# TensorE in a loop of 12 slots, with GpSimd's copies as its only wait

## The chip, the cores and the metric

The kernel runs on one core of one Trainium2 chip. The time is device microseconds of a whole execution. The execution from which the profile comes has its own time, which stands beside its span in the table below.

## The reference

128 batches of a 128 x 1024 float32 array are each multiplied by one of eight 128 x 128 matrices, picked by an index for each batch, and the product is added to the input.

```python
def reference(x, itok_B_0_7, L0_cond_weights):
    w = L0_cond_weights[itok_B_0_7]              # 128 x 128 x 128 from 8 x 128 x 128
    return x + jnp.einsum('bct,bcd->bdt', x, w)  # x: 128 x 128 x 1024 float32
```

The input and the output have 67.1 MB each, so some 134 MB go through the transfer engines.

## The kernel before

Two batches (G = 2) make one step of the main loop, 64 steps in all. A step has a slot `xs[k]` of 1 MB in SBUF (128 partitions x 2 x 1024 float32), and there are SLOTS = 23 slots, used in turn (k = i % SLOTS). The sum is written into the slot itself, so a slot is taken from the load of x until the store of the result has landed.

All instructions are written out in full, and the order on each engine is the order of the text. Semaphores alone tie the engines together:

- SyncE (SP) issues the load of the eight matrices (L130) and then 128 loads of 512 KB, two for each step, by the helper `transfer` (L57). For the first 23 steps a load waits until the load three steps earlier has landed (LEAD = 3); from then on it waits until the store out of the same slot has landed (`s_slot[k]`, which counts both loads and the store of each turn).
- GpSimd (POOL) reads eight indices at a time into registers (L155) and copies the matrix of each batch from `w_all` into one of four buffers `ws` (L165). It waits for `s_product`, so that a buffer is not overwritten while TensorE may still read it; so it runs up to four batches ahead.
- TensorE (PE) waits in each step for the loads of the slot (`s_slot[k]`), for the addition two steps earlier, which frees one of the two PSUM tiles (`s_added`), and in each batch for the copy of its matrix (`s_copied`). Then it does two products of 128x512 for each batch (L171). Its whole program, 256 products, is written out one after the other. Three products on zeros stand ahead of it (L114).
- VectorE (DVE) adds PSUM to the slot, one addition of 128x2048 for each step (L181). At the start it clamps the indices (L121 to L125).
- ScalarE (ACT) issues one store of 1 MB for each step, after the addition (L57 again, seen as ACTq).

The helper puts the transfers of SP and of ACT on one hardware queue each; in the profile q1 has the loads and q10 the stores. After its loads SP waits until the last store of every slot has landed (L192), and with that the kernel ends.

Of the kernel before, what the change touches and what calls it, by code (L numbers as in the profile page):

```python
# [1 line left out]

# [4 lines left out]

F32 = mybir.dt.float32
I32 = mybir.dt.int32
ALU = mybir.AluOpType


G = 2

N = 512  # L30

SLOTS = 23

W_SLOTS = 4
P_SLOTS = 2

R = 8
DMA = 16

TURN = DMA * (G + 1)  # L40

LEAD = 3

IDLE = 3

ROWS = 4
QUEUES = {mybir.EngineType.SP: "qSPDynamicHW", mybir.EngineType.Activation: "qActDynamicHW"}


def transfer(nc, engine, out, in_):  # L50

    later, nc._always_lower_symbolic_ap = nc._always_lower_symbolic_ap, False
    ins, outs = engine.lower_ap_dma(in_), engine.lower_ap_dma(out)
    nc._always_lower_symbolic_ap = later
    return engine.add_instruction(  # L57
        mybir.InstDMACopy(
            name=nc.get_next_instruction_name(),
            engine=engine.engine,  # L60
            ins=ins,
            outs=outs,
            mode="Copy",
            cce_op=ALU.bypass,
            queue=QUEUES[engine.engine],
        )
    )


@with_exitstack  # L70
def kernel(
    ctx: ExitStack,
    tc: tile.TileContext,
    x: bass.AP,
    subjects: bass.AP,
    weights: bass.AP,
    out: bass.AP,
):
    nc = tc.nc
    B, C, T = x.shape  # L80
    S, _, D = weights.shape
    NT = B // G

    def sbuf(name, *shape, dtype=F32):
        return ctx.enter_context(nc.sbuf_tensor(name, list(shape), dtype)).ap()

    given, near, wrap, index = (
        sbuf(name, 1, B, dtype=I32) for name in ("given", "near", "wrap", "index")
    )
    w_all = sbuf("w_all", C, S, D)  # L90
    ws = [sbuf(f"w{i}", C, 1, D) for i in range(W_SLOTS)]
    zeros = sbuf("zeros", C, N)
    xs = [sbuf(f"x{i}", C, G, T) for i in range(SLOTS)]
    ps = [
        ctx.enter_context(nc.psum_tensor(f"ps{i}", [D, G, T], F32)).ap() for i in range(P_SLOTS)
    ]

    s_given = tc.alloc_semaphore("s_given")
    s_wall = tc.alloc_semaphore("s_wall")
    s_index = tc.alloc_semaphore("s_index")  # L100
    s_zeros = tc.alloc_semaphore("s_zeros")
    s_copied = tc.alloc_semaphore("s_copied")
    s_product = tc.alloc_semaphore("s_product")
    s_added = tc.alloc_semaphore("s_added")
    s_slot = [tc.alloc_semaphore(f"s_slot{i}") for i in range(SLOTS)]

    with tc.tile_critical():  # L107

        nc.scalar.dma_start(given, subjects.rearrange("(o b) -> o b", o=1)).then_inc(s_given, DMA)

        nc.vector.memset(zeros, 0.0).then_inc(s_zeros, 1)  # L111
        nc.tensor.wait_ge(s_zeros, 1)
        for _ in range(IDLE):
            nc.tensor.matmul(  # L114
                ps[P_SLOTS - 1][:, G - 1, :N], zeros[:, :D], zeros, start=True, stop=True
            )

        nc.vector.wait_ge(s_given, DMA)  # L120
        nc.vector.tensor_scalar(near, given, -S, S - 1, ALU.max, ALU.min).then_inc(s_index, 1)  # L121
        nc.vector.wait_ge(s_index, 1)
        nc.vector.tensor_scalar(wrap, near, 0, S, ALU.is_lt, ALU.mult).then_inc(s_index, 1)  # L123
        nc.vector.wait_ge(s_index, 2)
        nc.vector.tensor_tensor(index, near, wrap, ALU.add).then_inc(s_index, 1)  # L125
        nc.gpsimd.wait_ge(s_index, 3)

        nc.sync.dma_start(w_all, weights.rearrange("s c d -> c s d")).then_inc(s_wall, DMA)  # L130
        for i in range(NT):
            k, turn = i % SLOTS, i // SLOTS
            if turn:
                nc.sync.wait_ge(s_slot[k], TURN * turn)
            elif i >= LEAD:
                nc.sync.wait_ge(s_slot[k - LEAD], DMA * G)
            for g in range(G):
                transfer(
                    nc,
                    nc.sync,  # L140
                    xs[k][:, g, :],
                    x[i * G + g].rearrange("(a r) t -> a (r t)", r=ROWS),
                ).then_inc(s_slot[k], DMA)

        nc.gpsimd.wait_ge(s_wall, DMA)
        for i in range(NT):
            k, turn = i % SLOTS, i // SLOTS
            p = ps[i % P_SLOTS]
            nc.tensor.wait_ge(s_slot[k], TURN * turn + DMA * G)
            if i >= P_SLOTS:  # L150
                nc.tensor.wait_ge(s_added, i - P_SLOTS + 1)
            for g in range(G):
                b = i * G + g
                if b % R == 0:
                    _, subject = nc.values_load_multi_w_load_instructions(  # L155
                        index[0:1, b : b + R],
                        engines=[mybir.EngineType.Pool],
                        min_val=0,
                        max_val=S - 1,
                        skip_runtime_bounds_check_because="the index is clamped on the chip above",  # L160
                    )
                w = ws[b % W_SLOTS]
                if b >= W_SLOTS:
                    nc.gpsimd.wait_ge(s_product, b - W_SLOTS + 1)
                nc.gpsimd.tensor_copy(w, w_all[:, bass.ds(subject[b % R], 1), :]).then_inc(  # L165
                    s_copied, 1
                )

                nc.tensor.wait_ge(s_copied, b + 1)
                for t in range(0, T, N):  # L170
                    mm = nc.tensor.matmul(  # L171
                        p[:, g, t : t + N],
                        w[:, 0, :],
                        xs[k][:, g, t : t + N],
                        start=True,
                        stop=True,
                    )
                mm.then_inc(s_product, 1)

            nc.vector.wait_ge(s_product, (i + 1) * G)  # L180
            nc.vector.tensor_tensor(xs[k], p, xs[k], ALU.add).then_inc(s_added, 1)  # L181
            nc.scalar.wait_ge(s_added, i + 1)
            transfer(
                nc,
                nc.scalar,
                out[i * G : (i + 1) * G].rearrange("g d t -> d g t"),
                xs[k].rearrange("d (o g) t -> d o (g t)", o=1),
            ).then_inc(s_slot[k], DMA)


        for i in range(NT - SLOTS, NT):
            nc.sync.wait_ge(s_slot[i % SLOTS], TURN * (i // SLOTS + 1))  # L192


# [1 line left out]
_INS = ["x", "itok_B_0_7", "L0_cond_weights"]  # L196
_OUTS = [((128, 128, 1024), "float32")]


# [20 lines left out]
```

## Time and profile before

| what | value |
|---|---|
| median of 3 runs | 327.43 us (327.18 to 327.75) |
| profiled execution, its own time | 327.53 us |
| span of the profiled execution | 325.5 us |
| moved by DMA | 134.85 MB, mean 414 GB/s |
| PE busy | 241.3 us (74%) |
| DVE busy | 147.9 us (45%) |
| POOL busy | 37.6 us (12%) |
| stores, median from issue to landing | 41.6 us |
| load halves, median from issue to landing | 11.8 us |
| packets of instructions on q8 and q14 | 4 (0.07 MB) and 4 (0.03 MB) |

An engine's busy time is the time in which it executed; the matmuls of TensorE overlap, so the mean of 607 ns that the profile gives for one is longer than the distance from one to the next. The slices of the profile cut the span into 40 equal parts, and each digit is the busy share in tenths. The chain of waits follows the end of the execution back; transfers hold most of it. In a line of waits the numbers are the total in us, how many there were, and the longest.

### The profile page before, as it was taken

The page shows a single profiled execution, that of the slowest core. Times are in us where ns is not written, and L with a number is a line of the kernel's source. Part 1 is how long each engine was busy: PE and PEld are TensorE (multiplying, and loading weights), DVE is VectorE, ACT ScalarE, POOL GpSimd, SP SyncE. Part 2 cuts the span into 40 slices and gives each one's busy share as a digit, 9 for nine tenths or more (in the row PEclk, how much of TensorE's full clock was granted, in tenths as well). Part 3 has the DMA queues.
Part 4 walks back from the last instruction along what each step waited for, and adds up shares of the span by engine and source line. Part 5 has one row for each costly group of instructions (what it writes and reads, how often), then busy time and mean ns, then how long its engine had stood idle before and what let it go on. Part 6 is the DMA issues. An engine that isn't in the chain of part 4 may idle for free.

```text
span 325.5 us, 1703 instructions
## 1 busy us (share of the span) xinstructions
PE 241.3 (74%) x518; PEld 95.2 (29%) x518; DVE 147.9 (45%) x68; POOL 37.6 (12%) x132
## 2 busy tenths in 40 slices
PE   6999998987989999989889889887777878000000
PEld 2444433332333333333333333332232332000000
DVE  1475765554555555555555555555354336100000
POOL 1111111111111111111111111111101110000000
PEclk9999999999999999999999999999999979755555
DMA  7999999999999999999999999999999999999994
GB/s 258 411 419 431 419 435 415 420 428 419 427 431 421 431 419 429 416 424 428 423 427 423 420 428 422 428 421 431 421 433 435 417 419 422 429 424 429 424 429 191
DMA packets 16410, 134.85 MB, mean 414 GB/s; under 512 B 3089, under 2 KB 4114, under 8 KB 4114
## 3 DMA queue, kind: packets, MB, share of 16 engines
q1 hardware_dynamic: 7184, 67.64, 49.6%
q10 hardware_dynamic: 9218, 67.11, 49.2%
q8 instruction: 4, 0.07, 0.1%
q14 instruction: 4, 0.03, 0.0%
HBM read 67.63 MB, written 67.11 MB: 414 GB/s over the span
## 4 chain that ended last, share of the span: by engine, by line
DMA 44%; SPq 23%; another core or an unknown queue 15%; PE 2%; issue 1%; DVE 1%
DMA x<-in_x_dram 29%; SPq L57 23%; DMA out_dram<-x 14%; PE ps L171 2%; DVE x L181 1%; SPq L130 0%; SPq L216 0%; SPq L107 0%
## 5 line engine op out<-in xcount | busy, mean ns | idle before, releaser
L171 PE MATMUL ps<-x,w 128*128 128x512 f32 x512 | 235.9, 607 | 32.5 <-DMA x<-in_x_dram 32.5
L181 DVE TENSOR_TENSOR x<-ps,x 128x2048 f32<-128x2048 f32 x64 | 146.7, 2292 | 128.0 <-PE ps L171 128.0
L171 PEld LDWEIGHTS ps<-x,w 128*128 128x128 f32 x512 | 93.4, 191 | 175.6 <-issue 97.3
L165 POOL COPY w<-w_all 128x128 f32 x128 | 37.4, 294 | 230.6 <-PE ps L171 224.6
L114 PE MATMUL ps<-zeros 128*128 128x512 f32 x6 | 5.4, 1076 | 1.7 <-DVE zeros L111 1.7
L114 PEld LDWEIGHTS ps<-zeros 128*128 128x128 f32 x6 | 1.8, 326 | 3.8 <-issue 2.1
L111 DVE MEMSET zeros<- 128x512 f32 x1 | 0.5, 485 | 1.1 <-SPq L107 1.1
L121 DVE TENSOR_SCALAR near<-given 1x128 int32<-1x128 int32 x1 | 0.2, 216 | 0.7 <-DMA given<-in_itok_B_dram 0.7
L125 DVE CUSTOM_DVE_ANT_0 index<-near,wrap 1x256 uint16<-1x256 uint16 x1 | 0.3, 280 | 0.0
L123 DVE TENSOR_SCALAR wrap<-near 1x128 int32<-1x128 int32 x1 | 0.2, 216 | 0.0
L207 POOL MEMSET const-float32-0.0<- 128x1 f32 x1 | 0.1, 98 | 0.2 <-issue 0.2
L207 POOL MEMSET const-bfloat16-1.0<- 128x1 bf16 x1 | 0.1, 101 | 0.0
L207 POOL MEMSET const-uint8-127<- 128x1 uint8 x1 | 0.1, 101 | 0.0
L207 POOL MEMSET const-float32-1.0<- 128x1 f32 x1 | 0.1, 98 | 0.0
## 6 DMA issues: line engine op xcount, KB each, us to landing
x<-in_x_dram SPq DMA_DIRECT2D x128, 512.0 KB, 11.8
out_dram<-x ACTq DMA_DIRECT2D x64, 1024.0 KB, 41.6
w_all<-in_L_cond_weights_dram SPq DMA_DIRECT2D x1, 512.0 KB, 4.4
given<-in_itok_B_dram ACTq DMA_DIRECT2D x1, 0.5 KB
```

The costliest lines, as they stand in the source:

```text
L57: return engine.add_instruction(mybir.InstDMACopy(name=nc.get_next_instruction_name(), engine=engine.engine, ins=ins, outs=outs, mode="Cop ...
L111: nc.vector.memset(zeros, 0.0).then_inc(s_zeros, 1)
L114: nc.tensor.matmul(ps[P_SLOTS - 1][:, G - 1, :N], zeros[:, :D], zeros, start=True, stop=True)
L121: nc.vector.tensor_scalar(near, given, -S, S - 1, ALU.max, ALU.min).then_inc(s_index, 1)
L123: nc.vector.tensor_scalar(wrap, near, 0, S, ALU.is_lt, ALU.mult).then_inc(s_index, 1)
L125: nc.vector.tensor_tensor(index, near, wrap, ALU.add).then_inc(s_index, 1)
L165: nc.gpsimd.tensor_copy(w, w_all[:, bass.ds(subject[b % R], 1), :]).then_inc(s_copied, 1)
L171: mm = nc.tensor.matmul(p[:, g, t : t + N], w[:, 0, :], xs[k][:, g, t : t + N], start=True, stop=True,)
L181: nc.vector.tensor_tensor(xs[k], p, xs[k], ALU.add).then_inc(s_added, 1)
L207: nc = _bacc.Bacc("TRN2", target_bir_lowering=False, num_devices=1)
```

## The change

The number of slots falls from 23 to 12, and TensorE's program becomes a loop: one body for 12 steps, run five times by a loop instruction of that engine alone, and then four more steps written out. For that, each turn of the loop has to be the same instructions with the same waits. So TensorE waits in a step only for `s_copied`, by the new helper `take`, which waits until the count is 2 and takes 2 off it. What TensorE waited for before, the landed loads of the slot and the addition two steps earlier, GpSimd now waits for ahead of the first copy of the step. The second copy of the step follows it. The four buffers `ws` hold the matrices of two steps, and as the addition two steps earlier comes after the products two steps earlier, the wait for `s_product` on GpSimd is gone. `s_product` now counts steps and not batches.

```diff
-SLOTS = 23
+SLOTS = 12
 W_SLOTS = 4
 P_SLOTS = 2
...
     )
+def take(engine, sem, count):
+    engine.sem_inc(sem, -count).wait_op(sem, count, "sem-ge")
 @with_exitstack
 def tile_subject_residual_kernel(
     ctx: ExitStack,
...
                     x[i * G + g].rearrange("(a r) t -> a (r t)", r=ROWS),
                 ).then_inc(s_slot[k], DMA)
+        def multiply(slots):
+            for k in slots:
+                take(nc.tensor, s_copied, G)
+                for g in range(G):
+                    for t in range(0, T, N):
+                        mm = nc.tensor.matmul(
+                            ps[k % P_SLOTS][:, g, t : t + N],
+                            ws[(k * G + g) % W_SLOTS][:, 0, :],
+                            xs[k][:, g, t : t + N],
+                            start=True,
+                            stop=True,
+                        )
+                mm.then_inc(s_product, 1)
+        with nc.tensor.Fori(0, NT // SLOTS):
+            multiply(range(SLOTS))
+        multiply(range(NT % SLOTS))
         nc.gpsimd.wait_ge(s_wall, DMA)
         for i in range(NT):
             k, turn = i % SLOTS, i // SLOTS
-            p = ps[i % P_SLOTS]
-            nc.tensor.wait_ge(s_slot[k], TURN * turn + DMA * G)
-            if i >= P_SLOTS:
-                nc.tensor.wait_ge(s_added, i - P_SLOTS + 1)
             for g in range(G):
                 b = i * G + g
                 if b % R == 0:
...
                         max_val=S - 1,
                         skip_runtime_bounds_check_because="the index is clamped on the chip above",
                     )
-                w = ws[b % W_SLOTS]
-                if b >= W_SLOTS:
-                    nc.gpsimd.wait_ge(s_product, b - W_SLOTS + 1)
-                nc.gpsimd.tensor_copy(w, w_all[:, bass.ds(subject[b % R], 1), :]).then_inc(
-                    s_copied, 1
+                if i >= P_SLOTS and g == 0:
+                    nc.gpsimd.wait_ge(s_added, i - P_SLOTS + 1)
+                copy = nc.gpsimd.tensor_copy(
+                    ws[b % W_SLOTS], w_all[:, bass.ds(subject[b % R], 1), :]
                 )
-
-                nc.tensor.wait_ge(s_copied, b + 1)
-                for t in range(0, T, N):
-                    mm = nc.tensor.matmul(
-                        p[:, g, t : t + N],
-                        w[:, 0, :],
-                        xs[k][:, g, t : t + N],
-                        start=True,
-                        stop=True,
-                    )
-                mm.then_inc(s_product, 1)
-
-            nc.vector.wait_ge(s_product, (i + 1) * G)
-            nc.vector.tensor_tensor(xs[k], p, xs[k], ALU.add).then_inc(s_added, 1)
+                if g == 0:
+                    copy.wait_op(s_slot[k], TURN * turn + DMA * G, "sem-ge")
+                copy.then_inc(s_copied, 1)
+            nc.vector.wait_ge(s_product, i + 1)
+            nc.vector.tensor_tensor(xs[k], ps[i % P_SLOTS], xs[k], ALU.add).then_inc(s_added, 1)
             nc.scalar.wait_ge(s_added, i + 1)
             transfer(
                 nc,
```

In the list of instructions TensorE's main program has 48 products in the loop and 16 after it, where it had 256; ACT, DVE, SP and GpSimd have one more branch each, to the block that follows the loop.

## The prediction

> **What bounds the kernel now.** I read the slices of the span first.
>
> ```profile
> PE   6999998987989999989889889887777878000000
> DVE  1475765554555555555555555555354336100000
> DMA  7999999999999999999999999999999999999994
> GB/s 258 411 419 431 419 435 415 420 428 419 427 431 421 431 419 429 416 424 428 423 427 423 420 428 422 428 421 431 421 433 435 417 419 422 429 424 429 424 429 191
> ```
>
> The sixteen DMA engines are busy in every slice but the first and last. TensorE and VectorE stop near 277 us, and for almost 50 us only transfers run. So I asked for stretches: reads almost alone, reads and writes under the start-up pacing, reads paced by stores, writes alone.
>
> ```profile
> core 0: us, PE busy (x) PEld busy (x) DVE busy (x) POOL busy (x), PEclk, DMA share, GB/s
> 8.00:14.00 6.00, 6.00 (x14) 2.74 (x15) 2.29 (x1) 0.88 (x3) 1.00 1.02 415
> 30.00:80.00 50.00, 45.15 (x101) 18.22 (x100) 28.67 (x13) 7.34 (x25) 1.00 1.01 424
> 210.00:260.00 50.00, 39.28 (x87) 15.29 (x85) 23.88 (x11) 6.16 (x21) 1.00 1.01 425
> 280.00:320.00 40.00, 0.00 (x0) 0.00 (x0) 0.00 (x0) 0.00 (x0) 0.50 1.01 426
> ```
>
> The last column is what matters: 424, 425 and 426 GB/s, whatever the mix. The page counts 134.85 MB, which at 425 GB/s is 317 us of the 325.5 us span. The rest is the start (first load issued at 1.5 us), the end (last store landed at 324.0 us) and differences between the engines. **The bytes set the time.**
>
> Next, where the slots sit. The queues in 30:80, then in 210:260:
>
> ```profile
> q1 hardware_dynamic: 1167, 12.80, 60.7%
> q10 hardware_dynamic: 1164, 8.39, 40.2%
> ...
> q10 hardware_dynamic: 1486, 10.85, 51.6%
> q1 hardware_dynamic: 955, 10.41, 49.4%
> ```
>
> q1 carries loads, q10 stores. While both have work, loads get 3 parts in 5 and stores fall behind. From about 205 us each load waits for the store that frees its slot, the rates become equal, and a slot (2 MB moved) takes 4.95 us. In that stretch a load half lands 7.6 us after its issue, and a 1 MB store 41.3 us. So most slots hold finished sums waiting to go out. The sync queue's waits say the same:
>
> ```profile
> SPq L57 <- DMA out_dram<-x: 97.5, 22, 5.1
> SPq L192 <- DMA out_dram<-x: 59.4, 11, 35.2
> ```
>
> Compute has room:
>
> ```profile
> L171 PE MATMUL ps<-x,w 128*128 128x512 f32 x512 | 235.9, 607 | 32.5 <-DMA x<-in_x_dram 32.5
> L181 DVE TENSOR_TENSOR x<-ps,x 128x2048 f32<-128x2048 f32 x64 | 146.7, 2292 | 128.0 <-PE ps L171 128.0
> L165 POOL COPY w<-w_all 128x128 f32 x128 | 37.4, 294 | 230.6 <-PE ps L171 224.6
> ```
>
> 607 ns overlaps; in the timeline the matmuls start 0.43 us apart and the eight records of a slot fill 3.70 us. When loads ran ahead at the start, additions came every 3.43 us. So compute can deliver a slot in 3.43 us, against the 4.95 us that DMA needs.
>
> Last, the end. The landing times of the last store's sixteen parts, counted from the first part (320.75 us), are 0, 0.10, 0.13, 0.14, 0.14, 0.22, 0.35, 0.44, 0.51, 0.72, 1.30, 1.60, 1.68, 2.00, 2.04 and 3.28 us. **One DMA engine is 3.28 us behind the first, and it alone sets the end.** Some of the others were held up by another traffic:
>
> ```profile
> q8 instruction: 4, 0.07, 0.1%
> q14 instruction: 4, 0.03, 0.0%
> ```
>
> The four q8 packets (16 KB each, at 73, 128, 185 and 256 us) come when 313, 536, 772 and 1036 of TensorE's 1108 records have begun, about 240 apart: its program arriving. After the packets at 73, 128 and 185 us, one part of each following store is late by 1.35 to 1.43 us more, each time another part. An 8 KB packet of q14 costs 0.56 to 0.80 us. The part that is last at the end was hit by none of these three; it was hit by the 8 KB packet at 125 us (+0.78 us), and for the rest it slipped by about 0.05 us from one store to the next as long as loads ran.
>
> [...] Here it fell once in mid-run, after an idle gap of 2.14 us at 262.6 us, for 3.4 us, and the following additions still fed a store queue with some 20 us or more of work. [...]
>
> **The change, part by part.** The sum is made against the profiled execution: 327.53 us, of which 325.5 is span and 2.0 lies around it. The median of the three runs is 327.43, 0.1 lower.
>
> *Bytes.* 128 load halves, 64 stores and the weights are unchanged: 0.
>
> *12 slots for 23.* Does DMA run dry? In the paced state a slot's round takes 12 x 4.95 = 59.4 us. The load takes about 8.6 us (both halves), compute 3.70 + 2.29 + 0.7 (below) = 6.7 us. What is left, 44 us or nine slots, waits as stores. The thinnest moment is when the pacing ends: load 12 needs store 0, which landed at 25.0 us, and may be issued at about 36 us; loads 13 and 14 need stores landing at 31.1 and 37.3 us. Then some five slots are loads, two compute, five stores: 5 MB, 12 us of writing. So DMA stays full: 0. The writes-alone end shrinks from some 50 us to about ten stores of 2.46 us; 25 us at 425 instead of 426 GB/s cost 0.06 us. The last slot still needs 6.7 us from its last load to its store, under that 25 us: 0.
>
> *GpSimd's copies behind the loads.* Before, four copies ran ahead and TensorE started 0.08 us after a landing. Now come first the copy (0.29), a register operation, the second copy (0.29) and the hand-over: I take 0.7 us per slot from the row of L165, at least 0.6, at most 1.2 if a load of eight indices (median 0.73 us, 16 times) isn't done ahead. Serial cost 64 x 0.7 = 45 us, hidden at 0 by 4.95 - 3.70 = 1.25 us of TensorE's slack per slot and by 44 us of waiting stores. Behind the waiting copy on GpSimd's queue stand only later copies and index loads. In the compute-paced first 30 us the copies of slot i wait for the addition of i-2, which ends about 2.4 us into the product of i-1; 0.7 more is 3.1 of 3.43 us. Before store 12 no load depends on it. Even a TensorE at half clock is bounded: its warm-up matmuls took 0.86 us each, 6.9 us a slot, and uninterrupted work restored the clock after 3.4 us. Cost 0; if the cover were gone, 0.7 us per slot.
>
> *Waits.* TensorE loses 64 load waits, 62 addition waits and 128 copy waits and gains 64 taking waits; the addition waits move to GpSimd; VectorE's count is one per slot as before. About 0.05 us each (the traced semaphore instruction is 51 ns), under the same slack: 0. The sync queue ends with 12 waits instead of 23, all but the last long satisfied: 0.
>
> *The loop.* A matmul is four records (two weight loads, two products), so a body is 48 x 4 + 12 = 204 records and the whole program about 290, below the 313 at which the first 16 KB packet came. I take no or one packet instead of four. Three or four times 1.4 us of single engines go, but not of the one that ends last: 0 gain. Lower bound for this part: -1.24 us, where the last engine falls back to the next (2.04). Upper bound: the branch back[...]. A stall of a few us per pass is hidden under the stores; the packets aren't, see below.
>
> Sum: 327.43 + 0.06, **327.5 us**.
>
> **Rivals.**
> *The end engine loses a delay (faster).* If the 8 KB packet meets another engine, or the slow slip shrinks with the other traffic, the end comes 0.78 us (that packet) to 1.24 us earlier: 326.65 to 326.2. For it: delays of the engines are the only loose time left. Against it: GpSimd's, ACT's, SP's and DVE's programs keep their length but for one branch, so their packets remain, and the slip went with the loads.
>
> *The branch back fetches the program anew (slower).* Five passes give 5 to 10 packets of 1.4 us. It decides from the first one on the last engine (328.9), or from the third on any one other (0.4 + 3 x 1.4 > 3.28). All of five on one engine: 0.4 + 7.0 - 3.28 = 4.1 us, 331.6. [...] Against it: the body is shorter than the 313 records run without a fetch before.
>
> *Twelve slots run dry.* It needs a stall of 12 us early or 40 us later; nothing above is over 7 us. At one lost slot time per pass: 5 x 4.95, 352 us. The change not doing what it says is one form of the second rival: a loop that saves no fetch.
>
> **How the numbers follow.** No change beyond 0.65 us (0.2%, about what a measurement of this kernel can tell from no change): 0.50. Faster by the end engine: 0.23. Slower: 0.27, of which 0.16 one refetch on the last engine or a little more slip (to 329.0), 0.08 piled refetches, 0.03 a dry pool. The range takes the faster case and the single refetch: 326.2 to 329.0, leaving out about 0.15.
>
> **What would show it.** Right: DMA nines to the end at 424 to 426 GB/s; TensorE working to about 305 us; GpSimd waiting for loads and TensorE for GpSimd; store latency about as before; at most one q8 packet; a spread of the last store's parts near 3 us. Wrong: a DMA slice below 9 in mid-run (a dry pool); five or more q8 packets (the loop refetches); a last spread of 2 us or less, or over 4 us.

## The result, and the profile after

The changed kernel takes 328.42 us (median of 8 runs, 328.28 to 328.75), the kernel before in the same comparison 327.44 us (8 runs, 327.18 to 327.75): slower by 0.98 us, ratio 1.0028, interval 1.0019 to 1.0038. In a second comparison on another chip (run e5 below) the loss was smaller: 328.28 against 327.65 us, ratio 1.0013, interval 1.0007 to 1.0020. The two kernels differ by 0.13 to 0.28%, with the changed one the slower in both.

The profiled execution took 328.28 us, of which 325.9 us are span and 2.4 us lie around it; before it was 327.53, 325.5 and 2.0. So a part of the loss is outside the span, where no row of the page can show it. The slices of the span after, TensorE, VectorE, GpSimd, the transfers and their rate:

```profile
PE   6999998888876866866866878678677686686200
DVE  1376665455544354354452525543534535435200
POOL 0111111111011011011010110110101101101000
DMA  7999999999999999999999999999999999999993
GB/s 255 412 411 429 423 428 423 425 421 433 417 428 429 416 438 415 426 433 418 424 428 422 427 424 424 433 422 421 426 424 430 429 416 433 420 424 425 426 424 148
```

The transfers are full in every slice but the first and last, as before. TensorE works to 304 us and no longer to 275. The stretches after (start, length, busy times by engine, clock, DMA share, GB/s in the last column):

```profile
30.00:80.00 50.00, 45.98 (x104) 18.46 (x102) 29.61 (x13) 6.36 (x24) 1.00 1.01 425
210.00:260.00 50.00, 36.81 (x81) 14.50 (x82) 22.30 (x11) 5.83 (x22) 1.00 1.01 426
260.00:300.00 40.00, 29.28 (x64) 11.39 (x65) 18.49 (x9) 4.24 (x16) 1.00 1.01 426
300.00:320.00 20.00, 3.67 (x8) 1.43 (x8) 3.12 (x2) 0.00 (x0) 0.69 1.01 426
```

The rate is that of before. The queues of the whole span after (packets, MB, share):

```profile
q1 hardware_dynamic: 7184, 67.64, 49.6%
q10 hardware_dynamic: 9218, 67.11, 49.0%
q14 instruction: 5, 0.03, 0.0%
```

The four packets of q8 are gone. The stretch from 326 to 330 us, behind the span, has one of them:

```profile
q8 instruction: 1, 0.02, 2.2%
q14 instruction: 1, 0.01, 0.9%
```

The 16 KB packet starts at 327.1 us, after the last instruction, and takes 1.4 us. In the kernel before only the 8 KB packet of q14 stands there. The groups of the main work, then the waits of the engines and of the sync queue (total us, times, longest us):

```profile
L159 PE MATMUL ps<-x,w 128*128 128x512 f32 x512 | 234.3, 604 | 62.2 <-PEq L74 62.2
L197 DVE TENSOR_TENSOR x<-ps,x 128x2048 f32<-128x2048 f32 x64 | 146.7, 2291 | 156.4 <-PE ps L159 156.4
L189 POOL COPY w<-w_all 128x128 f32 x128 | 33.9, 293 | 265.5 <-DMA x<-in_x_dram 241.3
```

```profile
POOL w L189 <- DMA x<-in_x_dram: 241.3, 56, 7.8
...
PE ps L159 <- PEq L74: 62.2, 53, 2.9
```

```profile
SPq L59 <- DMA out_dram<-x: 196.6, 49, 5.1
```

GpSimd now holds the wait for the loads, TensorE its wait in `take` (L74). The sync queue's waits for stores doubled from 97.5 to 196.6 us, since 49 loads and not 22 wait for the store of their slot. That GpSimd's waits cost nothing by themselves is shown by e2 below; what comes with fewer slots is asked by e1.

What moved inside the span stands in the landing times of the last store's sixteen parts. A store of 1 MB has 16 landings in the trace, and the page counts 16 DMA engines; that a part is the work of one engine is inferred from this, as no landing names its engine. The first part landed at 320.75 us before and at 320.41 us after; the last at 324.04 before and at 324.42 after. **The spread grew from 3.28 to 4.01 us.** The fifteen parts that land first became earlier in every rank (the fifteenth at 322.48 instead of 322.80 us), and the one that sets the end became later.

### The profile page after: what moved, and what is told of

It is laid out like the page before. It is cut to its first block, busy times and chain, and to the rows that moved or that the text cites. A ratio compares the mean times of both kernels' runs of the same rounds, so it can differ in the third digit from the quotient of the medians.

```text
span 325.9 us, 1709 instructions
## 1 busy us (share of the span) xinstructions
PE 239.8 (74%) x518; PEld 94.8 (29%) x518; DVE 147.8 (45%) x68; POOL 34.1 (10%) x132
## 5 line engine op out<-in xcount | busy, mean ns | idle before, releaser
L189 POOL COPY w<-w_all 128x128 f32 x128 | 33.9, 293 | 265.5 <-DMA x<-in_x_dram 241.3
## 6 DMA issues: line engine op xcount, KB each, us to landing
out_dram<-x ACTq DMA_DIRECT2D x64, 1024.0 KB, 43.6
```

What stands on the lines that cost most here:

```text
L189: copy = nc.gpsimd.tensor_copy(ws[b % W_SLOTS], w_all[:, bass.ds(subject[b % R], 1), :])
```

## The experiments

Each of the three groups ran beside its own runs of the kernel before. For the groups I also compare the mean span of all runs, and the mean of what lies around the span. The span's standard deviation was 0.2 to 0.6 us, so a difference of two mean spans is known to about 0.07 us, one standard error (0.08 in e2, 0.13 in e6, e7 and e9, 0.17 in e10). The ratio on record is not exactly that of the two medians given beside it. Every spread comes from one profiled execution. In the diffs "..." marks lines left out.

**e1: 12 slots alone.**

```diff
-SLOTS = 23
+SLOTS = 12
```

> The kernel before with 12 slots in place of 23 and nothing else: TensorE's program written out, its waits as they were. Three theories of the 0.98 us by which the changed kernel is slower (span +0.4 in the profile, the rest outside the span). SLOTS: with 12 slots loads are paced by stores from 75 us instead of 205 us, and in that stretch the last DMA engine slips more from store to store (0.065 us a step against 0.05 us per store before), so the last store's parts spread over 4.0 us and not 3.3: 327.9 to 328.2, span +0.5 to +0.8, four 16 KB packets on q8 still there. LOOP: the loop of TensorE makes the whole loss, by the block that it fetches after the end: this one 327.4, spread 3.3. WAITS: GpSimd's waits make it: also 327.4.

Measured: 327.89 us against 327.67 us, ratio 1.0005 (0.9997 to 1.0013). By the ratio alone the case is open. The total is at the low end of what SLOTS expected. The mean span was 325.92 us against 325.71 us, +0.21, far less than the 0.5 to 0.8 that SLOTS expected; 2.0 us lay around it, as before. The last store's parts in the profile ran from 320.36 to 324.77 us, a spread of 4.41. So 12 slots lengthen the span by about 0.2 us without any loop, and in this profile the spread was not the 3.3 us of the loop theory.

**e2: the new waits with 23 slots, written out.**

```diff
-SLOTS = 12
+SLOTS = 23
...
-                            xs[k][:, g, t : t + N],
+                            xs[k % SLOTS][:, g, t : t + N],
...
-        with nc.tensor.Fori(0, NT // SLOTS):
-            multiply(range(SLOTS))
-        multiply(range(NT % SLOTS))
+        multiply(range(NT))
```

> The changed kernel's waits (GpSimd alone waits for loads and additions, TensorE takes from the count of copies) with 23 slots and TensorE's program written out, no loop. SLOTS: 327.4, the spread of the last store's parts near 3.3 us, four packets on q8. LOOP: 327.4 too. WAITS: 328.0 or more.

Measured: 327.83 us against 327.67, ratio 1.0001 (0.9993 to 1.0009), mean span 325.58 us against 325.71, spread 3.44 us. The span is not longer, so GpSimd's waits cost nothing in it: WAITS has fallen. Around the span lay 2.19 us in the mean. The profile has three 16 KB packets in the span and one at 327.17 us, after its end, although nothing loops here.

**e3: the changed kernel without the loop, 12 slots.** The same edit of the loop, and SLOTS stays 12.

> The changed kernel with its 64 steps written out instead of the loop: 12 slots and the new waits remain. SLOTS: 327.9 to 328.2, with four packets on q8, the spread near 4 us, and 2.0 us outside the span (no packet of 16 KB after the end). LOOP: 327.4. WAITS: 328.0 or more. If it is at 328.4 or above with a spread as in the changed kernel, the loop has no part in the loss at all.

Measured: 328.12 us against 327.67, ratio 1.0011 (1.0004 to 1.0018), mean span 325.97 us (+0.26), around it 2.14 us, spread 3.98 us. The total and the spread are as SLOTS said; WAITS allowed this total too, but e2 has ruled it out. e2 and e3 differ in the number of slots alone, and their mean spans by 0.39 us. What SLOTS said of the packets and of the time outside the span is wrong: three packets came in the span, and the fourth at 326.99 us, after its end.

**e4: four turns of the loop, 16 steps written out.**

```diff
-                            xs[k][:, g, t : t + N],
+                            xs[k % SLOTS][:, g, t : t + N],
...
-        with nc.tensor.Fori(0, NT // SLOTS):
+        with nc.tensor.Fori(0, 4):
             multiply(range(SLOTS))
-        multiply(range(NT % SLOTS))
+        multiply(range(NT - 4 * SLOTS))
```

> The changed kernel with four turns of the loop and 16 steps written out after it, so that TensorE's program has about 495 records [...]. LOOP, that is the 16 KB packet of 1.4 us after the last store in the changed kernel: this packet comes earlier, the time outside the span falls from 2.35 to 2.0 us, total 328.1. SLOTS alone: the span stays at 326.1, and the total with it, 328.4, whatever the packet does. One packet on q8 inside the span at about 270 us in both.

Measured: 327.96 us against 327.67, ratio 1.0005 (0.9997 to 1.0013). The queues of its span:

```profile
q14 instruction: 4, 0.03, 0.0%
q8 instruction: 1, 0.02, 0.0%
```

The 16 KB packet came at 278.8 us, none after the end, and what lies around the span fell to 1.93 us (all 13 runs between 1.9 and 2.0). The span stayed long: 325.98 us, +0.27, spread 4.44. So in e1 to e4 there are **two losses, and they can be moved apart**: one in the span that goes with 12 slots, one around it that goes with the packet after the end. The total, 327.96 us, is below both cases expected.

**e5: the changed kernel again.**

> The changed kernel once more, on the chip on which the next ones run. So far: with 12 slots and no loop the span is longer by 0.2 to 0.3 us in the mean, and 0.15 to 0.35 us more lie outside the span where a 16 KB packet of q8 comes after the last store. If these two are all, the changed kernel is 0.5 to 0.6 us over the kernel before here (span +0.25, outside +0.33), a ratio of 1.0016 to 1.0019. If the loop costs something inside the span as well, its span is longer than that with 12 slots and no loop by over 0.15 us.

Measured: 328.28 us against 327.65 us (22 and 40 runs), ratio 1.0013 (1.0007 to 1.0020). Mean span 325.97 us against 325.72, +0.25: the same as e3 without a loop, so no cost of the loop shows in the span. Around it 2.20 us against 1.98, +0.22, and not the same in each run: 1.9 to 2.5 us in its 22 runs, while all 118 runs of the kernel before in these groups lie between 1.9 and 2.0. The sum of the two means, 0.47 us, is a little below the expected 0.5 to 0.6; the medians lie 0.63 us apart, and the ratio is below the expected 1.0016 to 1.0019.

**e6: the loop with 22 slots.**

```diff
-SLOTS = 12
+SLOTS = 22
```

> The changed kernel with 22 slots: the loop has 22 steps and runs twice, 20 steps follow it. TensorE's program has about 750 records, [...]. SLOTS plus END PACKET (the theory that the loss is 0.25 us in the span by 12 slots and 0.33 us outside by the packet after the end): both are gone, ratio 1.000 (0.999 to 1.001), spread of the last store's parts 3.3 us, 2.0 us outside the span. LOOP in itself: slower by 0.1% or more.

Measured: 328.05 us against 327.65, ratio 1.0011 (1.0003 to 1.0019), against expectation. Two q8 packets came in the span and none after it, as the 750 records let one estimate (in the kernel before 313, 536 and 772 records had begun at its first three packets), but around the span lay 2.2 us in each of the 17 runs, and the profiled execution (span 327.0 us, the slowest of the 17) had a spread of 4.58 us with 45 stores beside loads. The mean span, 325.86 us, scatters by 0.48 us, so its +0.14 tells little. Hence not all of the longer time around the span is this packet, and the spread varies between executions for reasons not found here.

**e7 and e9: the last store in two pieces.** The idea was to take work off the one engine that sets the end. That this split spares it, and the shares that it adds to the others, were the author's assumption and were not shown; the first case below holds if it spares it, the second if it doesn't.

```diff
+            for lo, hi in ((0, C),) if i < NT - 1 else ((0, 120), (120, C)):
                 transfer(
-                    out[i * G : (i + 1) * G].rearrange("g d t -> d g t"),
-                    xs[k].rearrange("d (o g) t -> d o (g t)", o=1),
+                    out[i * G : (i + 1) * G, lo:hi].rearrange("g d t -> d g t"),
+                    xs[k][lo:hi].rearrange("d (o g) t -> d o (g t)", o=1),
...
-            nc.sync.wait_ge(s_slot[i % SLOTS], TURN * (i // SLOTS + 1))
+            nc.sync.wait_ge(s_slot[i % SLOTS], TURN * (i // SLOTS + 1) + DMA * (i == NT - 1))
```

> The kernel before with the last store in two pieces, partitions 0 to 119 and 120 to 127. [...] the next one, at 2.0 us plus its added share of 0.2 to 0.5 us, sets the end: 0.8 to 1.0 us faster. If the last is another engine: 0.2 to 0.5 us slower[...].

Measured: 328.84 us against 327.65, ratio 1.0033 (1.0022 to 1.0044); slower by more than either case expected, the mean span by 1.18 us. The trace has 23 landings for the two pieces, where an undivided store has 16; it doesn't show on which engines they ran. The last came at 325.43 us. e9 turned the two pieces round:

> The kernel before with the last store in two pieces as in the run before, but the piece of 8 partitions (120 to 127) first and the 120 partitions after it. In the run before, the parts of the 120 partitions had all landed by 323.0 us, though the last engine's part of the store ahead of it landed at 321.9 and one more full part would have taken it to 324.4; the small piece, issued last, landed at 322.9 to 325.4 and set the end. If [...] only the place of the small piece was wrong: end at 323.0 to 323.6, span 0.5 to 1.0 us shorter than that of the kernel before, ratio 0.997 to 0.9985. If another engine is last: 326 us or more in the span as in the run before.

Measured: 328.40 us against 327.60, ratio 1.0022 (1.0013 to 1.0030), mean span 326.50 us (+0.83), last landing at 325.20 us in its profile. The order alone was not the fault. The span is as expected for the second case (326 us or more), but as no landing tells its engine, which one comes last stays open; splitting the last store this way made the end later in both orders (324.04 us in the kernel before).

**e8: loads alone for 100 us.** The loops over steps begin at step 40, and a load waits for a store only where the slot had one.

```diff
+FIRST = 40
...
-        for i in range(NT):
+        for i in range(FIRST, NT):
...
```

> The kernel before without the products, additions and stores of the first 40 steps (their part of the output isn't written): 100 us of loads alone at about 420 GB/s, then stores beside the last loads, then some 21 stores alone. It asks when the engine that comes last falls behind. If it slips with loads as such, the spread of a load's sixteen parts grows from under 1 us to 2 us or more over the first 40 loads. If it slips only where loads and stores mix, the spread stays as it is in the first 100 us, and the last store's parts are spread by 2 us or less, as only few stores go beside loads.

Measured, in a single execution: span 229.3 us. From load 1 to load 35 the spread of a second half's parts stayed at 1.13 us to the hundredth. Stretches of loads alone, mixed and stores alone:

```profile
10.00:100.00 90.00, 0.00 (x0) 0.00 (x0) 0.00 (x0) 0.00 (x0) 0.50 1.01 410
130.00:190.00 60.00, 56.97 (x130) 23.66 (x128) 36.95 (x17) 9.64 (x33) 1.00 1.01 425
200.00:225.00 25.00, 2.10 (x5) 0.57 (x3) 2.38 (x2) 0.00 (x0) 0.65 1.01 426
```

Eleven stores ran beside loads. Over the first eight their spread grew from 0.75 to 1.23 us, by 0.08 to 0.10 us from store to store in most of them, always by the last part. Over the next three it stood at 1.64 to 1.66, with a part in last place that a 16 KB packet of q8 at 174.9 us can have delayed, while the part behind it went on from 1.28 to 1.43. With stores alone the spread stood at 1.9 us. **In this run one engine falls further behind only while loads and stores run together.**

That is what 12 slots give more of: 55 stores have their first part landed before the last load lands, against 44 with 23 slots. From store 37 to 52 in the changed kernel the lag of the last part grew from 6.09 to 7.06 us, 0.065 us each (about 3 us of the lag go when the loads end, in both kernels). Eleven more stores would make 0.7 us by this estimate, beside the 0.73 by which the spread grew in the pair of profiles. The mean span grew by 0.25 only, and the spreads of single profiles overlap:

| run | slots | mean span less that of before, us | around the span, us | spread of the last store's parts, us | 16 KB packets in the span, after it |
|---|---|---|---|---|---|
| before | 23 | 0 | 1.98 to 1.99 | 3.28 | 4, 0 |
| changed, e5 | 12 | +0.25 | 2.20 | 4.06 | 0, 1 |
| e1 | 12 | +0.21 | 2.00 | 4.41 | 4, 0 |
| e2 | 23 | -0.13 | 2.19 | 3.44 | 3, 1 |
| e3 | 12 | +0.26 | 2.14 | 3.98 | 3, 1 |
| e4 | 12 | +0.27 | 1.93 | 4.44 | 1, 0 |
| e6 | 22 | +0.14 | 2.19 | 4.58 | 2, 0 |

In e7 and e9, which are the kernel before up to their last store, the store ahead of the last had a spread of 3.66 and 4.34 us. So with 12 slots it was 3.98 to 4.44, and with 22 or 23 from 3.28 to 4.58. That 12 slots lengthen the span is shown by the means; that they do it by the slip of this engine fits e8 and the count of stores, but isn't shown.

**e10: 6 slots.**

```diff
-SLOTS = 23
+SLOTS = 6
```

> The kernel before with 6 slots and nothing else. SLIP (the last engine loses 0.05 to 0.065 us with each store that goes out beside loads, nothing with stores or loads alone): with 6 slots 58 to 60 of the 64 stores go beside loads, instead of 53 with 12 slots and 43 with 23; so the last store's parts are spread by 4.3 to 4.8 us, the span is 0.3 to 0.6 us over that of the kernel before, ratio 1.001 to 1.002. POOL: a round of 6 slots takes 6 x 4.95 = 29.7 us, of which 15.3 are load and compute, so about three stores remain waiting and the transfers don't run dry; if they do, slices of the DMA row fall below 9 and the time rises by several us.

Measured: 328.37 us against 327.60, ratio 1.0029 (1.0018 to 1.0039), mean span +0.87 us. Stretches:

```profile
60.00:200.00 140.00, 105.12 (x225) 40.95 (x225) 64.24 (x29) 16.58 (x56) 0.99 1.01 425
200.00:300.00 100.00, 76.07 (x163) 29.63 (x162) 47.05 (x21) 11.85 (x40) 0.98 1.01 425
316.00:326.00 10.00, 1.67 (x4) 0.38 (x2) 2.29 (x1) 0.00 (x0) 0.72 0.54 222
```

Even six slots keep the transfers full in mid-run, as the count of slots in load, compute and store said. The slip was there: the last part of store 57 was 7.79 us behind the first. But the spread at the end was 0.36 us and not 4.3 to 4.8: the last load landed at 313.9 us, its sum was ready at 320.0, and there was no store left to cover all of that time (the store ahead had landed at 322.0), so the transfers paused before the last store and the lag was gone. With six slots another thing sets the end, so its time doesn't test the price of the slip.

## Why the prediction was right or wrong, point by point

The forecast was 327.5 us, no change, with 0.27 for slower. The measured 328.42 lies in the range, but by the prediction's own bound of 0.65 us (0.2%) the change is on the slower side in the first comparison and just under it in the second (0.63 us between the medians). So the likeliest case was not the right one in the first. That the time lies in the range is luck in part: its upper end came from a refetch on the last engine, which did not happen. Of the signs that it named, the full transfers, TensorE's end, the waits, the stores' latency and the packets came as said; the last spread, 4.01 us, was just over the 4 us that it had named as a sign of being wrong.

- *Bytes set the time, and the rate doesn't depend on the mix.* Right for the mixes in this pair, 425 and 426 GB/s in the stretches after; loads quite alone ran at 410 in e8.
- *12 slots don't let DMA run dry.* Right in its numbers: load 12 was issued at 35.7 us (36 expected), stores took 43.6 us (44), stores alone lasted 25 us, and e10 shows that half the slots would still keep the rate. **Wrong in its price.** The term was put at 0.06 us. It is about 0.25 us in the mean span (e1, e3, e4, e5: 0.21, 0.26, 0.27, 0.25), and 0.33 us in the pair of profiles. The prediction saw the slip of the last engine and wrote that it went on as long as loads ran, but left it out of this step, although fewer slots put eleven more stores beside loads. It took the end engine's lag as the same after without a reason. That the slip is what makes the 0.25 us fits e8 but isn't shown.
- *GpSimd's copies behind the loads.* Right. From the landing of the last load to TensorE's start were 0.73 us (0.7 expected; before it was mostly 0.05, not 0.08), to the end of the addition 6.73 us (6.7), and e2 puts the cost at nothing. TensorE's clock fell to half once in mid-run in both traces, each time for 3.4 us: in the kernel before at 262.9 us, just after the gap of 2.14 us, in the changed kernel at 191.7 us, just after one of 2.02 us. Gaps of 2.90 us (ended at 176.2 us) and 2.66 us (at 210.7 us) in the changed kernel left it at full, so what makes it fall isn't shown.
- *The waits.* Right, e2 too.
- *The loop.* One packet instead of four, as taken. That fewer packets would not move the end forward was right: the last part landed 0.38 us later. The first landed 0.34 us earlier, but so it did in e1 with all four packets (320.36 us), so this isn't the packets' doing. Doubtful is that the one packet costs nothing. It comes after the last store and is not under any cover; what lies around the span grew by 0.33 us in the first comparison and 0.22 in e5, and by nothing in e4, where the packet comes in mid-run. But e6 has 0.2 us more there without such a packet, so the packet is the likely cause and not a shown one. The sum had assumed the 2.0 us around the span unchanged without naming a reason.
- *The rival of the branch back.* It did not happen: with no q8 packet in the span, no turn is seen to fetch the loop again. That a branch back fetches at all, and so the 5 to 10 packets, was the author's assumption; the kernel before has no loop that could show it. The slower outcome came about otherwise than this rival said; only the words "a little more slip", a part of 0.16, name half of it.
- *The faster rival.* The opposite happened: the last part landed later.

The loss of the first comparison, 0.98 us, is larger than the two parts in e5, 0.25 + 0.22. In the first comparison the changed kernel had a mean span of 326.11 and 2.32 us around it, and the median of before less its 2.0 us is 325.4. The same two places hold it, with larger amounts. Why they are larger there is not settled. No version run here is faster than the kernel before; e4 has no loss after the end, and e2 shows that the waits alone are free in the span.

## What to carry to other kernels

Where transfers are full from start to end, ask which of the engines finishes last and what it alone does: here three packets of instructions fewer left the end no earlier. A pool that is deep enough to keep the rate may still be worth some of its depth (here 0.25 us for 23 slots over 12); it also decides how much of the writing is done alone (here the last 25 us with 12 slots, 52 with 23). Look also at what comes after the last instruction: a time that is measured holds more than the span, and a change of a program's length can move a packet of instructions from the middle to the end: here the last 16 KB packet came at 256 us before and at 327.1 us after, behind the last transfer, where it took 1.4 us.

## What the runs showed of the hardware that was not expected

- One DMA engine falls further behind only in mixed traffic: nothing in 35 steps of loads alone and in the stores alone (e8), 0.05 to 0.10 us with most 1 MB stores beside loads (the kernel before, the changed one, e8). Its cause, and which engine it is, stay open.
- In e8 loads alone ran at 410 GB/s, slower than loads and stores together (425) or stores alone (426), with the engines full in all three (share 1.01).
- Kernels whose profile has a 16 KB packet of q8 after the end have 1.9 to 2.5 us around the span from run to run (the changed kernel, e2, e3); the kernel before, e1, e4 and e10, which have none there, 1.9 to 2.0. The 22-slot loop has 2.2 us in every run with no such packet in its profile, which these runs don't explain.
